# Attention with residual on one core: the fourth query product by a second level of Strassen's scheme, and half of the last scores queued behind the values

## The chip, the cores and the metric

One core of a Trainium2 chip runs the whole program. The metric is the device time in microseconds (us) of one execution. The kernel before has a median of 1027.39 us over three runs (1027.23 to 1027.47). 0.2% of that, about what a measurement can tell from no change, is 2.05 us.

## The reference, cut to what is computed

Multi-query attention with 16 heads of 64 and one shared key/value head, over 64 batches of 128 tokens of 512 numbers, all float32, with a layernorm ahead and one behind, and the input added at the end:

```python
xn = layernorm(x, g_in)                                  # x: (64, 128, 512)
q = (xn @ Wq).reshape(b, n, 16, 64) * 64**-0.5           # Wq: (512, 1024)
k, v = split(xn @ Wkv)                                   # 64 + 64 columns
k, v = [null_k; k], [null_v; v]                          # one extra position
sim = einsum('bhid,bjd->bhij', q, k) + bias              # bias: (16, 128, 128) and a null column
attn = softmax(where(causal and not masked, sim, -big))
out = einsum('bhij,bjd->bhid', attn, v).reshape(b, n, 1024) @ Wo
x + layernorm(out, g_out)
```

## The kernel before, in words

**Work in steps.** The batches are taken in pairs, 32 steps `d` of two batches `a = 2d` and `b = 2d + 1`; four batches make a group `g`, so a group lasts two steps (`h = 0` in the even, `h = 1` in the odd one). A step is `turn(d)` (L956) followed by `body(d)` (L1245). `turn` puts out the scores of `a` and `b` (L652), adds the bias to them on DVE (L667) and multiplies the softmax of the pair before with its values (L781). `body` computes the keys and values (L363, `pkv`) and half of the queries of the group that comes next, the output projection of the pair before (L868, tiles `py`), the rest of the softmax (row maxima L674 on DVE, exponentials L683 on ACT, reciprocals L701 on DVE, scaling L705 on POOL, transposition in blocks of 32, `blocks_T`, L721 on DVE), and the outgoing layernorm of an earlier pair. Queries end with `d = 29`: `d = 30` and `31` are `turn_end` (L984) and `body_end` (L1099), and `turn_end(32)` with `body_last` (L1163) closes the program. Work of a group ahead of the first step is called the head, what stands behind `d = 29` the tail.

**What sets the order.** The schedule is written by hand: the order of the calls in the program is the order in each engine's queue. An engine takes its instructions in that order, and a later one does not pass one that waits. So moving a call moves its place on every engine that it uses, DMA issues on SP included.

**Query products.** `xn @ Wq` for a group is a product of two by two blocks: the token side is cut by batches (first two, last two) and by halves of the 512 inputs, the weight side by halves of the inputs and by halves of the 1024 outputs. Strassen's scheme in Winograd's form (`product`, L499) takes seven block products in place of eight, with sums of tokens (`token_sum`, on POOL, tiles `xS1` to `xS4`) and sums of weights (`wS`). One block product for 128 outputs (an `f`; two a step) is two matmuls of 256 columns. The seven go to the PSUM tiles `a` and `c`; ACT copies partial sums out (`keep`, L527), and DVE (`q_out`, L536) or ACT (`q_out` without a name, L533) writes the queries `qT`. Products 1, 6, 7 and 4 go to `a`, where 6, 7 and 4 are added to what stands there; 5 and 3 go to `c`.

**The second product** is already cut once more by the same scheme: `inner_product` (L565, matmul L581, tile `pl`) is seven single matmuls of 128 columns for both `f` of a step, in the PSUM tag `w`, and `inner_out` (L590, L597) seven additions of 128x128 on DVE. Its token sums `xL` come from POOL (L561) and its weight sums `wL` are made once.

**PSUM** has eight banks here: `s` (two), `a` and `c`, `X` and `Y`, and two of `w`. A tile that is allocated waits until the tile that had the bank has been read.

**Values.** `values` (L761) multiplies the transposed softmax with the values in four strips of 32 rows, each with its own quarter of the key positions and two column halves of the array, in four turns; a strip's matmul is 256 columns in the first turn and 128 in the other three. An argument `wide`, not used before, lets a strip take the two blocks of its third value tile as one matmul of 256 columns.

**Output projection.** `out_product` (L850) is the same scheme on the other side: products 1 to 7, each four matmuls of 256 columns, with sums made by `out_sum` (L848), and results put together by `out_keep` (L880) and `out_part` (L896, L898).

## Time and profile before

| | |
|---|---|
| median of three runs | 1027.39 us |
| time of the profiled execution | 1027.63 us |
| span in its trace | 1025.8 us |
| lies outside the span | 1.8 us |
| granted TensorE clock, mean | 0.999 |

In the profile every float32 matmul shows as two records, and so does its weight load; a group "x8" of L868 is thus one `out_product` of four matmuls. Where rows of matmuls follow one another, the time from one start to the next is what a group costs the queue; the second column is longer, because matmuls are pipelined and the last one's way through the array is counted. PE is the engine of the matmuls, PEld that of weight loads (beside PE), DVE, ACT and POOL work on vectors, SP issues DMAs. A bracket such as `[0.61 <-DVE oT L798]` says that the engine stood for 0.61 us ahead of the row and that the DVE instruction of line 798 ended this.

### The profile page before, as it was taken

To read this page: it belongs to the slowest core of one execution; us is meant where nothing else is said; L and a number is where in the kernel's file an instruction comes from. 1 tells how busy PE (TensorE), PEld (TensorE's weight loads), DVE (VectorE), ACT (ScalarE), POOL (GpSimd) and SP (SyncE) were. 2 spreads that over 40 slices of the span, in tenths; PEclk is the share of its full clock that TensorE was granted. 3 is DMA by queue.
4 is the path that set the end of the run, shared out by engine and by line. 5 is a ranking of instruction groups with operands and counts; after the bars stand their busy time and mean duration, and the time that the engine had idled before them with its cause. 6 is when DMAs were issued, how large, how long until landed. Compare 5 with 4: busy or idle time off the path is not lost.

```text
span 1025.8 us, 31271 instructions
## 1 busy us (share of the span) xinstructions
PE 1016.4 (99%) x12345; PEld 898.9 (88%) x12345; DVE 800.4 (78%) x1774; ACT 697.4 (68%) x2805; POOL 744.7 (73%) x579
## 2 busy tenths in 40 slices
PE   9999999999999999999999999999999999999997
PEld 9888888888888888888888888888888888888886
DVE  6877788877778877788777888777887777877697
ACT  5765678666677666786666776666776667856582
POOL 4997768676686867759677686766868678586676
PEclk9999999999999999999999999999999999999999
DMA  7415243051431414224052330514314152140211
GB/s 217 139 30 150 69 117 120 30 155 64 143 97 66 125 56 150 89 81 137 29 165 74 109 123 26 165 63 138 103 51 130 64 151 89 70 113 21 88 64 62
DMA packets 73833, 100.84 MB, mean 98 GB/s; under 512 B 32212, under 2 KB 36056, under 8 KB 71896
## 3 DMA queue, kind: packets, MB, share of 16 engines
q1 hardware_dynamic: 73392, 98.47, 30.9%
q8 instruction: 96, 1.57, 0.7%
q14 instruction: 49, 0.40, 0.1%
q10 hardware_dynamic: 296, 0.40, 0.1%
HBM read 63.19 MB, written 33.55 MB: 94 GB/s over the span
## 4 chain that ended last, share of the span: by engine, by line
PE 97%; DVE 1%; POOL 1%; issue 0%; POOLq 0%; DVEq 0%; ACT 0%
PE pa L515 20%; PE pyX L868 19%; PE pyY L868 10%; PE pc L515 10%; PE po L781 7%; PE pkv L363 6%; PE pyw L868 5%; PE pl L581 4%; PE pq L450 3%; PE ps L652 3%; PE sc_X L652 2%; PE sc_Y L652 2%; PE py_s L868 1%; PE sc_a L652 1%; PE busy L1453 1%; PE sc_w L652 1%
## 5 line engine op out<-in xcount | busy, mean ns | idle before, releaser
L683 ACT ACTIVATE s<-s,nmax 128x65 f32<-128x65 f32 (+1 forms) x1024 | 372.2, 368 | 62.1 <-DVE nmax L674 62.0
L705 POOL TENSOR_TENSOR s<-s,rinv 128x512 f32<-128x512 f32 (+1 forms) x132 | 190.6, 1446 | 159.9 <-DVE rinv L701 159.9
L617 POOL TENSOR_TENSOR s<-biasp,mneg 128x1552 f32<-128x1552 f32 (+1 forms) x65 | 206.0, 3171 | 51.1 <-DVE s L667 38.1
L683 ACT ACTIVATION_READ_ACCUMULATOR s<-s,nmax 128x1 f32 x1024 | 195.4, 191 | 0.0
L533 ACT COPY qT<-pa 128x256 f32<-128x256 f32 x59 | 22.0, 373 | 147.7 <-PE pa L515 147.7
L674 DVE TENSOR_REDUCE nmax<-s 128x8 f32<-128x1032 f32 (+1 forms) x128 | 121.4, 949 | 0.1
L515 PE MATMUL pa<-xS,wq 128*128 128x256 f32 x472 | 121.2, 379 | 0.0
L721 DVE STREAM_TRANSPOSE sb<-s 128x1536 f32<-128x1536 f32 (+1 forms) x68 | 113.5, 1672 | 2.0 <-POOL s L705 2.0
L868 PE MATMUL pyX<-wo,oT 128*128 128x256 f32 x464 | 109.7, 379 | 0.0
L868 PE MATMUL pyX<-wT,oT 128*128 128x256 f32 x464 | 109.7, 379 | 0.0
L515 PEld LDWEIGHTS pa<-xS,wq 128*128 128x128 f32 x472 | 87.3, 190 | 11.0 <-issue 0.2
L868 PEld LDWEIGHTS pyX<-wo,oT 128*128 128x128 f32 x464 | 86.0, 190 | 10.5
L868 PEld LDWEIGHTS pyX<-wT,oT 128*128 128x128 f32 x464 | 85.9, 190 | 10.6
L848 POOL TENSOR_TENSOR oT<-oT 128x512 f32<-128x512 f32 x64 | 80.5, 1276 | 3.9 <-PE pyw L868 1.6
L781 PE MATMUL po<-sb,vr 32*64 32x256 f32 (+1 forms) x4064 | 81.0, 300 | 0.0
L781 PEld LDWEIGHTS po<-sb,vr 32*64 32x64 f32 x4064 | 70.9, 130 | 8.1 <-issue 5.7
L536 DVE TENSOR_TENSOR qT<-pc,ku 128x256 f32<-128x256 f32 x118 | 48.6, 412 | 35.9 <-PE pc L515 20.8
L597 DVE TENSOR_TENSOR qT<-pl,kp 128x128 f32<-128x128 f32 x112 | 31.3, 280 | 55.5 <-PE pl L581 52.9
L800 ACT ACTIVATE oT<-po,nv 128x512 f32<-128x512 f32 (+1 forms) x127 | 73.8, 655 | 0.1
L281 POOL TENSOR_TENSOR rstd<-rstd,nhalf 128x1 f32<-128x1 f32 x64 | 35.0, 554 | 42.1 <-DVE rstd L280 39.2
L527 ACT COPY ku<-pa 128x256 f32<-128x256 f32 x118 | 43.4, 368 | 30.2 <-PE pa L515 26.2
L363 PE MATMUL pkv<-xT,wkv 128*128 128x256 f32 x256 | 63.3, 391 | 0.0
(186 smaller groups left out, 2418.9 us busy)
## 6 DMA issues: line engine op xcount, KB each, us to landing
res<-in_x_dram SPq DMA_DIRECT2D x64, 256.0 KB
x<-in_x_dram SPq DMA_DIRECT2D x63, 256.0 KB
out_dram<-y SPq DMA_DIRECT2D x63, 256.0 KB
xd<-xb SPq DMA_DIRECT2D x14, 1024.0 KB
xT<-xd SPq DMA_DIRECT2D x56, 256.0 KB
vr<-vd SPq DMA_DIRECT2D x64, 128.0 KB
kT<-kT SPq DMA_DIRECT2D x32, 64.0 KB
vd<-vb SPq DMA_DIRECT2D x32, 64.0 KB
```

Of the source, the lines that this page charges most:

```text
L363: nc.tensor.matmul(pkv, wkv[:, kc, :], xT[g][:, t : t + 2, kc, :], start=(kc == 0), stop=(kc == KC - 1),)
L515: nc.tensor.matmul(prod[tag], w[:, kc, f * P : (f + 1) * P], t[:, :, kc, :], start=(start and kc == 0), stop=(kc == HK - 1), skip_group_ch ...
L617: nc.gpsimd.tensor_tensor(S[b][:, :, keys], biasp[:, :, keys], mneg[:, t, keys] .unsqueeze(1) .broadcast_to([P, R8, keys.stop - keys.start ...
L652: nc.tensor.matmul(home[r][u * DH : (u + 1) * DH, f, :], qT[g, f, t // 2][rows, t % 2, hf, u], kT[rows, 0 : nk // Q, t, :], start=True, st ...
L674: nc.vector.tensor_reduce(nmax[b][:, hf], S[b][:, :, WITH_NULL[hf]], AX.X, ALU.max, negate=True)
L683: nc.scalar.activation(row, row, AF.Exp, bias=nmax[b][:, hf, k : k + 1], accum_out=rsum[b][:, hf, k : k + 1],)
L705: nc.gpsimd.tensor_tensor(sv, sv, rinvs[b, hf][:, lo:hi].unsqueeze(2).broadcast_to([P, hi - lo, sv.shape[2]]), ALU.mult,)
L721: nc.vector.transpose(sbs[b][:, :, lo:hi].rearrange("p j e q -> p e j q"), S[b][:, lo:hi, 1 : ROW - 1].rearrange("p e (j k) -> p e j k", k=Q),
L781: nc.tensor.matmul(po[s][rows, to : to + n], vr[g][quad, t, PLACE[j], :], sb[quad, slots, r * NF : (r + 1) * NF, :], start=(turn == 0), st ...
L800: nc.scalar.activation(to, src, AF.Identity, bias=nv2)
L848: eng.tensor_tensor(o, a, b, op)
L868: nc.tensor.matmul(prod[key], h[:, c, :], w[:, c, :], start=(start and c == 0), stop=(c == HC - 1), skip_group_check=not start,)
```

## The change

Four things change, and some memory is rearranged for them.

**1. The fourth product of steps 4 to 29 is cut once more.** For both `f` of a step, `product(g, f, 4)` (two matmuls of 256 columns each, added in the bank `a`, then an ACT copy to `qT`) goes. In its place stand seven matmuls of 128 columns (`last_product`, L647 of the kernel after, tile `pm`, in the two banks `s`), each of them a product of token sums and weight sums, and seven additions of 128x128 on DVE (`last_out`, L663). The partial result that was in the bank is now taken from the copies that `keep` had already made (`base`). In each even step POOL makes four more token sums (`token_sums_last`, tile `xM` and one block of `xS4` in place), and DVE makes four weight sums once, in steps 2 and 3.

**2. Calls are reordered around it.** `product(g, f1, 1)` moves up to where product 4 of `f0` stood. Products 5 and 3 of `f1` change places with output products 5 and 7. `scale(a, 1)` stands ahead of `values_T`.

**3. Wide values.** In `turn` of steps 5 to 29, strip 3 of `values(p)` takes its third value tile as one matmul of 256 columns; `values(p + 1)` does in odd steps and in those with `d % 10 == 4`.

**4. The last steps.** In `turn_end` of 30 and 31 the second half of the scores of `b` moves from ahead of the values to behind them, with other PSUM banks; `exps(a, 0)` is cut at 4 of 8 heads, with `scores_max(b, 0)` and `out_sum(p, 0)` between. In `body_end` of 30 the second half of `blocks_T(b)` no longer waits for the next turn, and two `late_gain` go from DVE to POOL.

Besides: one `x` tile fewer is loaded ahead (`XB`), the mask tile of a group has one buffer and its load moves from the even to the odd step, and the head computes one of its query blocks as four matmuls of 256 columns (`q_half(7, 0)`) where it had eight of 128.

```diff
+    def last_product(g, h, k):
+        if k == 1:
+            last_in[g, h] = ps_s.tile([P, 2, DIM], FP, tag="s", name=f"pm_{g}_{h}")
+        b, x = xS[g, 4], xM[g]
+        w, t, at = {
+            1: (g11, b[:, 0, 0], 0),
+            2: (g12, b[:, 0, 1], 2),
+            3: (v4, b[:, 1, 1], 1),
+            4: (g22, x[:, 2], 0),
+            5: (v1, x[:, 0], 1),
+            6: (v2, x[:, 1], 0),
+            7: (v3, b[:, 1, 0], 0),
+        }[k]
+        nc.tensor.matmul(last_area(g, h, at), w[:, h], t, start=k in (1, 2), ...)
+    def last_out(g, h, f, t, at, first=False):
+        o = q_part(g, HC + 2 * h + f, 0)[:, t]
+        p = last_area(g, h, at).rearrange("p (h i) -> p h i", h=2)
+        k = o
+        if first:
+            k = base[f].rearrange("p (t h i) -> p t h i", t=2, h=2)[:, t]
+        nc.vector.tensor_tensor(o, p, k, ALU.add)
...
-        values(p)
-        values(p + 1)
+        values(p, WIDE if 4 < d < PAIRS - 1 else ())
+        values(p + 1, WIDE if 4 < d < PAIRS - 1 and (d % 2 or d % 10 == 4) else ())
...
-        scores(b, 1, ((ps_y, "X"), (ps_q, "c")))
...
-        po = values_rooms(p)
+        values_rooms(p, ((ps_q, "c"), (ps_w, "w"), (ps_y, "X"), (ps_w, "w")))
         values(p)
         values(p + 1)
+        scores(b, 1, ((ps_y, "Y"), (ps_q, "a")))
...
         if soft:
             scale(b, 0)
+        if sums and d > 2:
+            token_sums_last(g)
...
-        if q:
+        if deeper:
+            product(g, f1, 1, ps_q, "a")
+        elif q:
             product(g, f0, 4, ps_q, "a", start=False)
             q_out(g, HC + f0, 0, "a")
...
+        if deeper:
+            product(g, f1, 3, ps_q, "c", start=False)
+            q_out(g, f1, 1, "c", "u2")
+            last_product(g, h, 3)
+            last_product(g, h, 4)
+            last_out(g, h, 1, 0, 0, True)
+            last_out(g, h, 0, 1, 1)
         if soft:
             blocks_T(b)
-        if q:
+        if q and not deeper:
             product(g, f1, 4, ps_q, "a", start=False)
             q_out(g, HC + f1, 0, "a")
```

**How the queues change.** A row below is one instruction or a run of equal ones ("x2"); the figures in a name are group, `f` or `h`, product and a running number. First TensorE's queue in the middle of the odd step of group 12 (`d = 23`), before: `pl` is the second product, `pa` and `pc` the block products, `pyY` the output product 5.

```order
L581 MATMUL pl_12_1_9996<-xT_12_9254,wq_81 128x128
L515 MATMUL pa_12_2_1_9989<-xS4_12_9616,wq_81 128x256 x2
L515 MATMUL pc_12_2_5_10031<-xT_12_9254,wS_139 128x256 x2
L515 MATMUL pa_12_3_1_10089<-xT_12_9254,wq_81 128x256 x2
L581 MATMUL pl_12_1_9996<-xL_12_9559,wq_81 128x128
L515 MATMUL pc_12_3_5_10116<-xS1_12_9520,wS_139 128x256 x2
L868 MATMUL pyY_44_5_10119<-wT_141,yS_44_10011 128x256 x4
L515 MATMUL pa_12_3_1_10089<-xS2_12_9522,wS_139 128x256 x2
```

The same place after; `pm` is the new tile:

```order
L581 MATMUL pl_12_1_10155<-xT_12_9396,wq_81 128x128
L515 MATMUL pa_12_3_1_10222<-xT_12_9396,wq_81 128x256 x2
L515 MATMUL pc_12_2_5_10190<-xT_12_9396,wS_138 128x256 x2
L647 MATMUL pm_12_1_10250<-xS4_12_9763,wq_81 128x128 x2
L581 MATMUL pl_12_1_10155<-xL_12_9708,wq_81 128x128
L936 MATMUL pyY_44_5_10277<-wT_140,yS_44_10170 128x256 x4
L515 MATMUL pc_12_3_5_10284<-xS1_12_9669,wS_138 128x256 x2
L515 MATMUL pa_12_3_1_10222<-xS2_12_9671,wS_138 128x256 x2
L581 MATMUL pl_12_1_10155<-xL_12_9708,wq_81 128x128
L581 MATMUL pl_12_1_10155<-xT_12_9396,wL_139 128x128
L647 MATMUL pm_12_1_10250<-xM_12_9805,wM_92 128x128 x2
```

The product of `xS4` for `f = 2` (two matmuls of 256) is gone; `pa` of `f = 3` stands in its place, two `pm` matmuls of 128 follow, and the output product 5 passes ahead of `pc` of `f = 3`.

Second, DVE's queue at the end of the same step, before (`sb` is the transposed softmax, and the last row is the first score addition of the next step):

```order
L536 TENSOR_TENSOR qT_12_3_1_9947<-pc_12_3_5_10116,ku3_10153 128x4x64
L898 TENSOR_TENSOR y_44_10049<-pyY_44_5_10119,kyu2_10146 128x256
L536 TENSOR_TENSOR qT_12_3_1_9947<-pc_12_3_5_10116,ku2_10129 128x4x64
L904 BN_STATS sto_44_10166<-y_44_10049 128x6
L906 BN_AGGR mvo_44_10168<-sto_44_10166 128x2
L908 TENSOR_SCALAR rstdo_44_10170<-mvo_44_10168 128x1
L898 TENSOR_TENSOR y_45_10177<-pyX_44_1_10013,kyp5_10124 128x256
L721 STREAM_TRANSPOSE sb_47_10179<-s_47_9745 128x8x6x32
L667 TENSOR_TENSOR s_48_9928<-sc_48_0_w_10190,s_48_9928 128x4x64
```

After:

```order
L536 TENSOR_TENSOR qT_12_3_1_10104<-pc_12_3_5_10284,ku3_10317 128x4x64
L663 TENSOR_TENSOR qT_12_3_0_10103<-pm_12_1_10250,ku3_10317 128x2x64
L663 TENSOR_TENSOR qT_12_3_0_10103<-pm_12_1_10250,qT_12_3_0_10103 128x2x64
L966 TENSOR_TENSOR y_44_10208<-pyY_44_5_10277,kyu2_10310 128x256
L972 BN_STATS sto_44_10330<-y_44_10208 128x6
L974 BN_AGGR mvo_44_10332<-sto_44_10330 128x2
L976 TENSOR_SCALAR rstdo_44_10334<-mvo_44_10332 128x1
L966 TENSOR_TENSOR y_45_10341<-pyX_44_1_10172,kyp5_10282 128x256
L536 TENSOR_TENSOR qT_12_3_1_10104<-pc_12_3_5_10284,ku2_10290 128x4x64
L663 TENSOR_TENSOR qT_12_3_0_10103<-pm_12_1_10250,ku3_10317 128x2x64
L663 TENSOR_TENSOR qT_12_2_0_10101<-pm_12_1_10250,qT_12_2_0_10101 128x2x64
L787 STREAM_TRANSPOSE sb_47_10350<-s_47_9905 128x8x6x32
```

Four of the seven additions of a step now stand here, and the second addition from `pc` has moved behind the last one of the output (`y_45`), so that three instructions stand between that and the transposition.

Third, TensorE's queue in `turn_end` of step 30, before (`ps` and `sc` are scores, `po` the values' results):

```order
L652 MATMUL ps_60_1_12618<-kT_138,qT_15_3_0_12370 64x128 x4
L652 MATMUL sc_61_1_X_12635<-kT_138,qT_15_0_0_11991 64x128 x2
L652 MATMUL sc_61_1_c_12636<-kT_138,qT_15_0_0_11991 64x128 x2
L652 MATMUL sc_61_1_X_12635<-kT_138,qT_15_1_0_11993 64x128 x2
L652 MATMUL sc_61_1_c_12636<-kT_138,qT_15_1_0_11993 64x128 x2
L652 MATMUL sc_61_1_X_12635<-kT_138,qT_15_2_0_12368 64x128 x2
L652 MATMUL sc_61_1_c_12636<-kT_138,qT_15_2_0_12368 64x128 x2
L652 MATMUL sc_61_1_X_12635<-kT_138,qT_15_3_0_12370 64x128 x2
L652 MATMUL sc_61_1_c_12636<-kT_138,qT_15_3_0_12370 64x128 x2
L781 MATMUL po_58_0_12662<-sb_58_12531,vr_14_11736 64x2x128 x2
```

After:

```order
L849 MATMUL po_58_2_12861<-sb_59_12792,vr_14_11938 64x128 x2
L849 MATMUL po_58_3_12862<-sb_59_12792,vr_14_11938 64x128 x2
L718 MATMUL sc_61_1_Y_12927<-kT_137,qT_15_0_0_12189 64x128 x2
L718 MATMUL sc_61_1_a_12928<-kT_137,qT_15_0_0_12189 64x128 x2
L718 MATMUL sc_61_1_Y_12927<-kT_137,qT_15_1_0_12191 64x128 x2
L718 MATMUL sc_61_1_a_12928<-kT_137,qT_15_1_0_12191 64x128 x2
L718 MATMUL sc_61_1_Y_12927<-kT_137,qT_15_2_0_12576 64x128 x2
L718 MATMUL sc_61_1_a_12928<-kT_137,qT_15_2_0_12576 64x128 x2
L718 MATMUL sc_61_1_Y_12927<-kT_137,qT_15_3_0_12578 64x128 x2
L718 MATMUL sc_61_1_a_12928<-kT_137,qT_15_3_0_12578 64x128 x2
L936 MATMUL py_58_1_s_12984<-wo_90,oT_58_12952 128x256 x4
```

The sixteen `sc_61_1` matmuls now stand between the last matmul of the values and the first output product, `py_58_1_s` (`py_s` in the profile).

More of the change, by code (lines that the diff above doesn't have):

```diff
@@ L597, in inner_out, with weight_sums_last, token_sums_last, last_area @@
         nc.vector.tensor_tensor(o, p, k, ALU.add)
+    in_last = a22.rearrange("p k (h f m) -> p k f h m", h=2, f=2)
+    g11, g12 = in_last[:, 0, 0], in_last[:, 1, 0]
+    g21, g22 = in_last[:, 0, 1], in_last[:, 1, 1]
+    v1, v2 = (wM[:, i * 2 * P : (i + 1) * 2 * P] for i in range(2))
+    v1, v2 = (v.rearrange("p (h m) -> p h m", h=2) for v in (v1, v2))
+    v4, v3 = wR, g21
+    xM, last_in, base = {}, {}, {}
+    def weight_sums_last(*ks):
+        for k in ks:
+            o, p, m, op = {
+                1: (v1, g21, g22, ALU.add),
+                2: (v2, v1, g11, ALU.subtract),
+                4: (v4, g12, v2, ALU.subtract),
+                3: (v3, g11, g21, ALU.subtract),
+            }[k]
+            nc.vector.tensor_tensor(o, p, m, op)
+    def token_sums_last(g):
+        b = xS[g, 4]
+        x = xM[g] = gp.tile([P, 3, N], FP, tag="xM", name=f"xM_{g}", bufs=1)
+        for o, p, m in (
+            (x[:, 0], b[:, 1, 0], b[:, 0, 0]),
+            (b[:, 1, 0], b[:, 1, 1], b[:, 1, 0]),
+            (x[:, 1], b[:, 1, 1], x[:, 0]),
+            (x[:, 2], b[:, 0, 1], x[:, 1]),
+        ):
+            nc.gpsimd.tensor_tensor(o, p, m, ALU.subtract)
+    def last_area(g, h, at):
+        two = last_in[g, h]
+        return two[:, 0, 0:N] if at == 0 else two[:, 1, (at - 1) * N : at * N]
+    def last_product(g, h, k):
[10 more added lines that the diff above has]
+            7: (v3, b[:, 1, 0], 0),
+        }[k]
+        nc.tensor.matmul(
+            last_area(g, h, at),
+            w[:, h],
+            t,
+            start=k in (1, 2),
+            stop=True,
+            skip_group_check=k not in (1, 2),
+        )
+    def last_out(g, h, f, t, at, first=False):
[5 more added lines that the diff above has]
+        nc.vector.tensor_tensor(o, p, k, ALU.add)
     S, nmax, rsum = {}, {}, {}
@@ L1154, in body_end @@
         blocks_T(b, *lo)
-        late_T.append((b, *hi))
+        if last:
+            late_T.append((b, *hi))
+        else:
+            blocks_T(b, *hi)
+            for m in (l, l + 1):
+                late_gain(m, nc.gpsimd)
+                late_residual(m, nc.gpsimd)
         out_product(p, 4, ps_s, "s", start=False)
         out_part(p + 1, 0, "s")
-        if not last:
-            for m in (l, l + 1):
-                late_gain(m)
-                late_residual(m, nc.gpsimd)
     def body_last():
@@ L1255, in body @@
         deep = q and d > 1
+        deeper = q and d > 3
         if q:
@@ L1384, in body @@
             weight_sums_inner()
[L1385 to L1386 removed]
+        if d == 2:
+            weight_sums_last(1, 2, 4)
         if soft:
@@ L1391, in body @@
             exps(b, 1, 0, 2)
-        if q:
+        if q and h == 1:
+            values_T(g)
+        if q and not deeper:
             product(g, f1, 5, ps_q, "c")
@@ L1396, in body @@
             out_keep("Y", "yp5", "yp5")
+        if deeper:
+            product(g, f1, 5, ps_q, "c")
         if soft:
@@ L1406, in body @@
             inner_out(g, h, 0, 1, 1)
+        if deeper:
+            last_product(g, h, 6)
+            last_product(g, h, 5)
+            last_out(g, h, 0, 1, 0, True)
         if soft:
@@ L1425, in body @@
             out_part(p, 1, "Y", "yu2")
-        if q:
+        if q and not deeper:
             product(g, f1, 3, ps_q, "c", start=False)
```

69 lines of the change are left out of this document (40 added, 29 removed).

## The prediction

> **What bounds the kernel now.** I read the page first: the span, the busy shares, the granted clock and the shares of the chain that ended last.
>
> ```profile
> span 1025.8 us, 31271 instructions
> ...
> PE 1016.4 (99%) x12345; PEld 898.9 (88%) x12345; DVE 800.4 (78%) x1774; ACT 697.4 (68%) x2805; POOL 744.7 (73%) x579
> ...
> PEclk9999999999999999999999999999999999999999
> ...
> PE 97%; DVE 1%; POOL 1%; issue 0%; POOLq 0%; DVEq 0%; ACT 0%
> ```
>
> TensorE is busy 99% of the span and holds 97% of the chain, at a full clock from end to end. An average can hide stages, so next I cut two neighbouring steps out of the middle, each from one key/value product (`pkv`) to the next. The columns are the sum of the engine work in PE, PEld, DVE, ACT and POOL, then clock and DMA.
>
> ```profile
> 504.08:535.31 31.23, 31.23 (x388) 27.64 (x383) 25.00 (x57) 21.26 (x87) 21.69 (x16) 1.00 0.42 126
> 535.31:566.53 31.22, 31.22 (x386) 27.62 (x382) 24.27 (x56) 22.27 (x89) 23.60 (x20) 1.00 0.21 73
> ```
>
> PE works 31.23 of 31.23 us and 31.22 of 31.22: no wait is left in a step. Every other engine has four us or more to spare. So inside a step only the length of TensorE's own queue counts, as long as no other engine becomes late. That makes the forecast a count of matmuls, plus a search for new waits.
>
> **Part 1, the fourth product: what it costs on TensorE.** The timeline of PE in the first of these steps gives the price of both sizes. The columns are start and length; the queue's price is the distance between starts.
>
> ```profile
> 513.04 0.61 PE L581 MATMUL pl<-xL,wL 128*128 128x128 f32 x4
> 513.49 0.39 PE L581 MATMUL pl<-xT,wq 128*128 128x128 f32 x2
> 513.71 1.03 PE L515 MATMUL pa<-xS,wq 128*128 128x256 f32 x4
> 514.58 1.03 PE L515 MATMUL pc<-xT,wS 128*128 128x256 f32 x4
> 515.44 1.03 PE L515 MATMUL pa<-xT,wq 128*128 128x256 f32 x4
> 516.30 0.38 PE L581 MATMUL pl<-xL,wq 128*128 128x128 f32 x2
> ...
> 519.98 0.38 PE L581 MATMUL pl<-xL,wq 128*128 128x128 f32 x2
> 520.20 0.39 PE L581 MATMUL pl<-xT,wL 128*128 128x128 f32 x2
> 520.42 1.89 PE L868 MATMUL pyX<-wT,oT 128*128 128x256 f32 x8
> ...
> 527.33 1.03 PE L515 MATMUL pa<-xS,wq 128*128 128x256 f32 x4
> 528.20 1.89 PE L868 MATMUL pyX<-wT,oT 128*128 128x256 f32 x8
> ```
>
> Twelve records of 256 columns run from 513.71 to 516.30: 2.59 / 12 = 0.216 us each. Ten of 128 columns take 513.71 − 513.04 = 0.67 and 520.42 − 519.98 = 0.44, so 1.11 / 10 = 0.111 us each. The fourth product is the row at 513.71 for the first `f` and the one at 527.33 for the second: 8 records, 8 × 0.216 = 1.73 us of a step. In its place come seven matmuls, 14 records: 14 × 0.111 = 1.55 us. The saving is 0.173 us a step, and in 26 steps (4 to 29) **4.5 us**. A cut into seven of eight would save an eighth, 0.216; the small size gives 0.043 of that back.
>
> Do these small matmuls cost 0.111 here too? Their weight loads last longer than that:
>
> ```profile
> L581 PEld LDWEIGHTS pl<-xL,wq 128*128 128x128 f32 x112 | 21.3, 190 | 2.9
> ```
>
> 190 ns each, but the ten records above come 111 ns apart with these loads, so loads overlap one another, and `last_product` has the same sizes. I take 0.111, with bounds of 0.110 (the 0.44 over four) and 0.112 (the 0.67 over six), ± 0.014 a step, ± 0.4 us in all.
>
> **Part 1 elsewhere.** DVE gets seven additions a step, ACT loses two copies, POOL gets four subtractions in every second step:
>
> ```profile
> L597 DVE TENSOR_TENSOR qT<-pl,kp 128x128 f32<-128x128 f32 x112 | 31.3, 280 | 55.5 <-PE pl L581 52.9 <-ACT kp L527 1.8
> L533 ACT COPY qT<-pa 128x256 f32<-128x256 f32 x59 | 22.0, 373 | 147.7 <-PE pa L515 147.7
> L561 POOL TENSOR_TENSOR xL<-xT,xL 128x128 f32<-128x128 f32 x14 | 6.4, 457 | 1.1
> ```
>
> DVE: 7 × 0.28 = 1.96 us on top of 25.00, under 27 of 31.2. ACT: 2 × 0.373 = 0.75 less. POOL: 4 × 0.457 = 1.83 on top of 23.60, in an even step. All three keep 4 us or more, so only their places in the order can hurt. The tightest is the end of a step on DVE and POOL's `scale(b, 0)` in the even one:
>
> ```profile
> 527.53 0.42 DVE L898 TENSOR_TENSOR y<-pyX,kyp 128x256 f32<-128x256 f32 x1 [0.30 <-PE pyX L868]
> 527.88 1.77 DVE L721 STREAM_TRANSPOSE sb<-s 128x1536 f32<-128x1536 f32 x1
> ...
> 530.78 0.42 DVE L667 TENSOR_TENSOR s<-sc_w,s 128x256 f32<-128x256 f32 x1 [1.14 <-PE sc_w L652]
> ```
>
> ```profile
> 547.75 1.04 POOL L705 TENSOR_TENSOR s<-s,rinv 128x512 f32<-128x512 f32 x1
> 550.01 1.91 POOL L705 TENSOR_TENSOR s<-s,rinv 128x1024 f32<-128x1024 f32 x1 [1.21 <-DVE rinv L701]
> ```
>
> In the changed queue one output product stands between the last `pm` matmul and the scores, as the row at 528.20 does now. So the last `pm` leaves the queue at about 528.20 and is through the array 0.39 − 0.22 = 0.17 later, at 528.37; the last addition ends at 528.65 and the transposition at about 530.4, where it now ends at 529.65. The next score addition starts at 530.78 because of its matmul, and was idle for 1.14 us before that. About 0.35 us of it is left: no wait for PE. Behind that addition are the other scores, whose PSUM banks `w` the values need. What is queued behind a late transposition is just that, so each us beyond the 0.35, and beyond what the values leave, would be one of TensorE's. POOL's 1.83 us start where `scale(b, 0)` ends (551.92) and fall partly into the idle time that `scale(a, 1)` has ahead of it, as `scale(b, 0)` has 1.21; DVE transposes `a` after it, for values that come in the next step. `pm` needs `xM` only with its third matmul, 2 × 0.22 and a `pl` and two larger products later. I count nothing for these, and bound it by rival A.
>
> **Part 3, wide values.** Here a matmul of 256 columns replaces two of 128 in strip 3: 4 records fewer per call, 25 calls for `p` (steps 5 to 29) and 15 for `p + 1` (13 odd steps, 14 and 24), 40 calls.
>
> ```profile
> L781 PE MATMUL po<-sb,vr 32*64 32x128 f32 x3048 | 60.8, 271 | 0.0
> L781 PE MATMUL po<-sb,vr 32*64 32x256 f32 x1016 | 45.4, 389 | 0.0
> ```
>
> ```profile
> 501.63 2.52 PE L781 MATMUL po<-sb,vr 32*64 32x256 f32 x128
> 504.08 1.99 PE L363 MATMUL pkv<-xT,wkv 128*128 128x256 f32 x8
> ```
>
> A pair takes 504.08 − 501.63 = 2.45 us for 128 records. The eight corners of the array run side by side, and each has per batch 2 records of 256 and 6 of 128: 2 × 2 × 0.216 + 12 × 0.111 = 2.20 us for two batches. So columns explain 2.20 of 2.45, and the number of columns does not change. At most the remaining 0.25 comes from the count of records, 2.45 / 128 = 0.019 each, which would be 0.077 per call; at least nothing. I take the middle, 0.035 per call, as both limits are about equally near: 40 × 0.035 = **1.4 us** (0 to 3.1). What could be below nothing is rivals B and C.
>
> **Part 4, the tail.** The only other waits of PE that the change touches are these, before the first output product of the last two turns:
>
> ```profile
> PE py_s L868 <- DVE oT L798: 1.4, 2, 0.8
> ```
>
> ```profile
> 970.01 2.52 PE L781 MATMUL po<-sb,vr 32*64 32x256 f32 x128
> 973.14 1.97 PE L868 MATMUL py_s<-wo,oT 128*128 128x256 f32 x8 [0.61 <-DVE oT L798]
> ...
> 988.90 0.35 ACT L683 ACTIVATE s<-s,nmax 128x65 f32<-128x65 f32 x1 [2.87 <-DVE nmax L674]
> ...
> 992.00 1.97 PE L868 MATMUL py_s<-wo,oT 128*128 128x256 f32 x8 [0.79 <-DVE oT L798]
> ...
> 1002.61 0.80 ACT L1090 ACTIVATE y<-y,lnm,lrs 128x512 f32<-128x512 f32 x1
> ...
> 1003.66 1.91 DVE L721 STREAM_TRANSPOSE sb<-s 128x768 f32<-128x768 f32 x2
> ...
> 1005.62 0.45 PE L781 MATMUL po_s<-sb,vr 32*64 32x256 f32 x4
> ```
>
> Half of the scores of `b` now run in these waits of 0.61 and 0.79. But the last values (1005.62) start when the last transposition ends (1003.66 + 1.91 = 1005.57), and that is the end of ACT's exponentials, begun at 988.90 after a row maximum of the first scores of step 31. Those come 0.61 earlier at best, by the first wait; the second is off the path. `scores_max(b, 0)` and `out_sum(p, 0)` now stand between parts of the exponentials' inputs and outputs, which may cost some of it. I take **0.5 us**, between a loss of 0.3 and a gain of 1.4 (both waits). For the rest I count nothing: the head block has the same columns in fewer matmuls; the four weight sums (4 × 0.42 at most, as the 128x256 addition at 527.53) fall once into DVE's 6 us of idle time in a step; the mask load stands on SP behind the step's only reader of its one buffer, ahead of `x` loads that are needed a step later.
>
> **Sum.** 1027.63 − 4.5 − 1.4 − 0.5 = 1021.2 for the profiled execution; it lay 0.24 above the median of the runs, so **1021.0**. The bounds together: 4.9 + 3.1 + 1.4 gives 1018.0, and 4.1 + 0 − 0.3 gives 1023.6.
>
> **Rivals.**
>
> *A: the new additions make TensorE wait.* If DVE's end of a step is late by more than the 0.35 us and the slack of the banks, each step loses again what it won. For it: DVE's end of step has three instructions more ahead of a 1.77 us transposition. Against it: no PE wait for DVE is in either window. With 0.173 a step lost: 1027.4 − 1.4 − 0.5 = **1025.5**. Chance 0.09.
>
> *B: the wide matmul of strip 3 holds the other strips.* The queue's later records are for strips 0 to 2, which have finished with their 128 columns when strip 3 is in its second 128. If these must stand until strip 3 is through, both of its records cost the difference of the two rows above, 389 − 271 = 118 ns: 0.236 per call, 40 × 0.236 = 9.4 us. Time: 1027.4 − 4.5 − 0.5 + 9.4 = **1031.8**, slower. It decides from 5.0 / 40 = 0.125 us per call. For it: no row of before has records of both sizes in one turn. Against it: 128 records of 271 or 389 ns each go through in 2.45 us, so corners do run beside one another, and strip 3's second record has only to have started, not ended, for the queue to move on. Chance 0.07.
>
> *C: matmuls end in order.* If a short record may not end before a long one ahead of it, only the second record of strip 3 delays what follows, once per call: 40 × 0.118 = 4.7 us, time 1027.4 − 4.5 − 0.5 + 4.7 = **1027.1**, no change. No row of before shows a short record behind a long one. The Trainium skill has this rule, which speaks against the change: "TensorE: Matmul & The Clock Gate", Part 3: Packing small matmuls — row/col tiling, The mechanism, says that matmuls keep program order in start and in end. Chance 0.045.
>
> *D: it doesn't do what it says*, the small matmuls paying their whole load of 190 ns: 14 × 0.19 − 1.73 = 0.93 us a step more, 26 × 0.93 = 24 us, **1049**. The `pl` rows speak against it. Chance 0.02.
>
> **How the numbers follow.** The forecast has 0.775. A lies at the bound of 0.2% (2.05 us, about what a measurement of this kernel can tell from no change; 1025.3), so half of it counts as faster, half as the same. Faster: 0.775 + 0.045 = 0.82; same: 0.045 + 0.045 = 0.09; slower: 0.07 + 0.02 = 0.09. The range holds the forecast's bounds except their last few tenths below, and reaches up to A: 1018.6 to 1025.5.
>
> **What would show it.** `pm` rows 0.22 apart per two records, and `pkv` rows 31.05 instead of 31.23 apart, less up to 0.1 by the values, whose 2.45 becomes some 2.38. No PE row with idle time that DVE `qT` or `s`, or POOL `xM`, ended; such rows would be A. Values that last 2.6 or 2.7 in odd steps would be C or B. In the tail, `py_s` without its 0.61 and 0.79, and the last values about 6 us earlier than 1005.62. The prediction is wrong at its root if the distance of `pkv` rows does not shrink.

## The result, and the profile after

The changed kernel takes 1023.07 us (median of six runs, 1022.52 to 1023.66) where the kernel before takes 1027.41: a ratio of 0.9957, 95% interval 0.9946 to 0.9968. That is 4.3 us less; the forecast was 6.4 less (1021.0, range 1018.6 to 1025.5). The profiled executions differ by 1027.63 − 1022.89 = 4.74 us, and this is the difference that the views below take apart.

The page of the kernel after:

```profile
span 1021.0 us, 31459 instructions
...
PE 1013.0 (99%) x12333; PEld 901.6 (88%) x12333; DVE 845.7 (83%) x1958; ACT 673.2 (66%) x2753; POOL 768.6 (75%) x633
...
q8 instruction: 96, 1.57, 0.6%
...
PE 97%; POOL 1%; DVE 1%; issue 0%; ACT 0%; POOLq 0%; DVEq 0%
```

TensorE still sets the time. The row `q8` is new to the argument: it is the queue that brings TensorE's instructions, 96 packets of 1.57 MB / 96 = 16.4 KB. TensorE has 2 × 12,333 records (matmuls and weight loads), so a packet holds 24,666 / 96 = 257 of them; I take 256 below, and the places at which packets come will bear that out.

Two neighbouring steps without a stop (TensorE standing still in the middle of the values), and the two that had one (step 4, ending at 159.96, and step 16, ending at 533.00), in the columns of the prediction:

```profile
564.08:595.17 31.09, 31.09 (x390) 27.75 (x385) 26.73 (x64) 20.30 (x85) 20.77 (x16) 1.00 0.45 129
595.17:626.25 31.08, 31.08 (x386) 27.72 (x381) 25.96 (x63) 21.31 (x87) 26.12 (x24) 1.00 0.22 72
128.59:159.96 31.37, 31.37 (x388) 27.78 (x383) 25.45 (x58) 21.39 (x88) 21.84 (x16) 1.00 0.43 127
501.86:533.00 31.14, 31.14 (x391) 27.62 (x385) 26.78 (x64) 20.35 (x85) 20.85 (x16) 1.00 0.43 125
```

A step went from 31.225 to 31.09 and 31.08, where the forecast said 31.05 less up to 0.1. PE's share cannot show the stops, because the last group's modelled end covers them; the length of the window does: 31.37 and 31.14.

The new matmuls, the end of a step on DVE, and one pair's values with the key/value product that follows:

```profile
917.35 0.61 PE L647 MATMUL pm<-xS,wq 128*128 128x128 f32 x4
917.80 0.39 PE L581 MATMUL pl<-xL,wq 128*128 128x128 f32 x2
...
934.61 2.54 PE L849 MATMUL po<-sb,vr 32*64 32x256 f32 x120
937.07 1.13 PE L363 MATMUL pkv<-xT,wkv 128*128 128x256 f32 x4
```

```profile
930.35 0.28 DVE L663 TENSOR_TENSOR qT<-pm,qT 128x128 f32<-128x128 f32 x1
930.55 1.77 DVE L787 STREAM_TRANSPOSE sb<-s 128x1536 f32<-128x1536 f32 x1
932.53 0.42 DVE L733 TENSOR_TENSOR s<-sc_w,s 128x256 f32<-128x256 f32 x1 [0.21 <-PE sc_w L718]
```

`pm` costs (917.80 − 917.35) / 4 = 0.112 us a record, as forecast. The transposition ends at 932.32 and the score addition still waits for its matmul, with 0.21 us of idle time left (0.35 was forecast): DVE delays nobody. The values of this pair take 937.07 − 934.61 = 2.46 us, not less than the 2.45 of before.

The waits of PE in the whole program (the first row is the start):

```profile
PE busy L1556 <- POOL neg L245: 1.4, 1, 1.4
PE py_s L936 <- DVE rinv L767: 0.7, 2, 0.4
PE pyc L936 <- DVE y L966: 0.6, 1, 0.6
```

`py_s` before the first output products no longer waits for `oT`; two smaller waits, 0.28 and 0.38 us, stand at other places of the tail. And one wait of before is missing that the prediction did not speak of. In step 1, before and after:

```profile
85.15 1.89 PE L868 MATMUL pyY<-wo,oT 128*128 128x256 f32 x8
87.49 1.13 PE L515 MATMUL pc<-xT,wS 128*128 128x256 f32 x4 [0.45 <-DVE qT L536]
```

```profile
85.08 1.89 PE L936 MATMUL pyY<-wo,oT 128*128 128x256 f32 x8
86.80 1.03 PE L515 MATMUL pc<-xT,wS 128*128 128x256 f32 x4
```

From `pyY` to `pc` it was 2.34 us and is 1.72. On DVE the reciprocal of `a` now passes `values_T`, a transposition of 0.71 us; POOL's scaling, `blocks_T` and the addition that frees the bank `c` all come 0.9 us earlier.

**The first account.** By the starts of `pkv` the kernel after is 0.78 us ahead at step 2, and the steps and the tail give the rest. A theory from these views: the cut product gives what was forecast, wide values cost a little, the head and the tail give about 0.7 and 0.5. Its rivals stand with each run. The first runs showed that it lacked the most important thing.

### The profile page after: what moved, and what is told of

It reads as the page before. It is cut to its first block, busy times and chain, and to the rows that moved or that the text cites. A ratio compares the mean times of both kernels' runs of the same rounds, so it can differ in the third digit from the quotient of the medians.

```text
span 1021.0 us, 31459 instructions
## 1 busy us (share of the span) xinstructions
PE 1013.0 (99%) x12333; PEld 901.6 (88%) x12333; DVE 845.7 (83%) x1958; ACT 673.2 (66%) x2753; POOL 768.6 (75%) x633
## 3 DMA queue, kind: packets, MB, share of 16 engines
q8 instruction: 96, 1.57, 0.6%
## 4 chain that ended last, share of the span: by engine, by line
PE 97%; POOL 1%; DVE 1%; issue 0%; ACT 0%; POOLq 0%; DVEq 0%
PE pyX L936 20%; PE pa L515 16%; PE pyY L936 10%; PE pc L515 10%; PE po L849 8%; PE pkv L363 6%; PE pyw L936 5%; PE pl L581 4%; PE pm L647 4%; PE ps L718 3%; PE pq L450 3%; PE sc_X L718 2%; PE sc_Y L718 2%; PE sc_a L718 1%; PE py_s L936 1%; PE busy L1556 1%
## 5 line engine op out<-in xcount | busy, mean ns | idle before, releaser
L964 ACT COPY y<-pyX 128x256 f32<-128x256 f32 x29 | 10.8, 372 | 167.5 <-PE pyX L936 161.2
L849 PE MATMUL po<-sb,vr 32*64 32x128 f32 (+1 forms) x3904 | 81.8, 308 | 0.0
L515 PE MATMUL pa<-xS,wq 128*128 128x256 f32 x264 | 67.8, 380 | 0.0
L515 PE MATMUL pa<-xT,wq 128*128 128x256 f32 x236 | 60.6, 380 | 0.0
```

Source lines behind the costliest of these rows:

```text
L515: nc.tensor.matmul(prod[tag], w[:, kc, f * P : (f + 1) * P], t[:, :, kc, :], start=(start and kc == 0), stop=(kc == HK - 1), skip_group_ch ...
L849: nc.tensor.matmul(po[s][rows, to : to + n], vr[g][quad, t, PLACE[j], :], sb[quad, slots, r * NF : (r + 1) * NF, :], start=(turn == 0), st ...
```

## The experiments

Every run is measured against the kernel before on the same chip (medians 1027.41 to 1027.55). A stop, below, is time by which the values of a pair of batches take longer than 2.47 us, counted where they take over 2.50; without one they take 2.45 with plain and 2.47 to 2.48 with wide values.

### Without wide values

```diff
-    WIDE = (3,)
+    WIDE = ()
```

Expected: 

> The changed kernel with no wide values. Theory (read from the trace after: values last 2.466 us in steps with two wide calls and 2.479 in those with one, against 2.450 before): wide values cost 0.016 to 0.029 us a step, and without them each pair takes 2.45 again; 14 x 0.016 + 11 x 0.029 = 0.5 us less, 1022.5. Rival (the prediction's term): wide values save 0.035 us a call, and the busier DVE makes the pairs long; without them each pair takes over 2.50 and the time is 1024.4.

Measured: 1030.83 us (ratio 1.0031, interval 1.0021 to 1.0042), 7.8 us slower than with them, which neither theory allowed. Two steps of this kernel, and the values in the second:

```profile
191.62:222.68 31.06, 31.06 (x393) 27.68 (x389) 26.72 (x64) 20.27 (x85) 20.76 (x16) 1.00 0.47 128
600.61:632.31 31.70, 31.45 (x391) 27.81 (x389) 26.09 (x63) 21.54 (x87) 25.50 (x25) 1.00 0.23 71
```

```profile
597.50 1.37 PE L849 MATMUL po<-sb,vr 32*64 32x256 f32 x59
599.14 1.54 PE L849 MATMUL po<-sb,vr 32*64 32x128 f32 x69 [0.27 <-issue]
600.61 1.56 PE L363 MATMUL pkv<-xT,wkv 128*128 128x256 f32 x6
```

Some steps take 31.06, shorter than any of the changed kernel; others 31.7, and then TensorE stands in the middle of the values for "issue": it waits for nothing that the profile shows. In the waits this is

```profile
PE po L849 <- issue: 2.4, 7, 0.7
...
PE pkv L363 <- issue: 0.5, 1, 0.5
```

and by the lengths of all pairs, 18 of 29 have a stop, 8.5 us in all (one more, of 0.75 us, falls into a `pkv`). Within the turn a stop's place moves back by 12 to 14 records from step to step (record 503 in one, 489 and 477 in the next two; 373, 359 and 347 later), and it ends 1.2 to 1.5 us after a `q8` packet has landed. So TensorE had run out of instructions at the border of a packet. New theory: **the program of a step has to keep the packets' borders where the next packet comes in time.** Counted in the program's order (two records and two loads for each matmul), a step of the kernel before has 764 instructions, near three packets of 256. Seven matmuls of 128 for four of 256 make 776; wide values take 16 or 8 away: 760 and 768, about 764 on average.

This count leaves out TensorE's semaphore instructions, which the trace also has: 8 in two steps of the kernel before, 10 in two of the changed kernel. With them a step of the kernel before has 764 + 4 = 768, exactly three packets, and its packets do come at the same place of every step: the third starts 27.4 to 28.2 us after the start of the values in each of the steps 2 to 28. A step of the changed kernel without wide values has 776 + 5 = 781, 13 more than three packets, which is the 12 to 14 by which the stops move.

### Without the cut product

```diff
-        deeper = q and d > 3
+        deeper = False
```

(and none of its sums). Expected: 

> The changed kernel with the fourth product as it was before (two matmuls of 256 columns a step and f, ACT copies, none of the new sums), wide values, tail and the other orders kept. Theory: the body of a step is 0.164 us longer again in 26 steps, 4.3 us, and the stop of 0.14 us in step 4 goes: 1023.1 + 4.3 - 0.1 = 1027.2. Rival: the cut product gives less than that in the body because its additions delay something, and the time rises by 3 us or less, to 1026.

Measured: 1033.95 us (1.0060, 1.0046 to 1.0074), again far outside both. Its steps have 748 or 756 instructions, and 16 pairs have stops, 4.6 us in all, with wide values in place. So it isn't the form of the values that makes or mends a stop.

### The old tail

The functions `turn_end` and `body_end` are those of before. Expected: 

> The changed kernel with the last two steps (turn_end, body_end) as they were before. Theory: the waits of 0.61 and 0.79 us ahead of the first output product come back, of which the end feels 0.5: 1023.6. Rivals: the end feels both, 1.4 us, 1024.5; or nothing, since the exponentials set the end, 1023.1.

Measured: 1023.49 (0.9960, 0.9948 to 0.9973), 0.42 more; the wait of `py_s` for `oT` is back with 1.3 us in two. A difference this small lies within the two kernels' spreads, and the traces put the tail lower: from the `pkv` of step 29 to the start of the last matmul it takes 78.41 us here and 78.14 in the changed kernel, 0.27 us. The rest of what the profiled executions differ by, 1023.76 − 1022.89 = 0.87, is mostly stops: in steps 2 and 4 the values take 2.93 and 2.86 us here, 2.45 and 2.59 there, although the program is the same up to step 29. So stops at these two steps come and go from one execution to the next.

### The old order of values_T

```diff
+        if q and h == 1:
+            values_T(g)
         if soft:
             exps(a, 1, 4)
             rinv(a, 1)
             scale(a, 1)
             exps(b, 1, 0, 2)
-        if q and h == 1:
-            values_T(g)
```

Expected: 

> The changed kernel with values_T ahead of rinv(a, 1) and scale(a, 1) again, in every odd step. Theory: in step 1 the 0.71 us transposition of values_T delays the reciprocal, POOL's scaling, the transposition blocks_T and the addition that frees the bank c, so PE waits about 0.6 us again there, and in the other steps nothing changes: 1023.8. Rival: the head's gain of 0.7 us is from the changed head block or the mask load, and the time stays at 1023.1; or each odd step of the changed kernel needs the new order, 13 x 0.5 us, 1029.

Measured: 1024.27 (0.9967, 0.9955 to 0.9980), 1.2 more (1.6 in the profiled executions). The wait in step 1 is back:

```profile
87.21 1.13 PE L515 MATMUL pc<-xT,wS 128*128 128x256 f32 x4 [0.44 <-DVE qT L536]
```

and in this execution step 2 had a stop in the values as well (2.97 us in place of 2.45), and another of about 0.55 us came in the values of step 31. Without its stop, the way from the `pkv` of step 1 to that of step 2 is 32.62 − 0.52 = 32.10 us, as in the kernel before (32.10), where the changed kernel takes 31.39. The head's gain is this order, 0.71 us in step 1 alone.

### Wide values on the kernel before

```diff
-        values(p)
-        values(p + 1)
+        values(p, (3,) if 4 < d < PAIRS - 1 else ())
+        values(p + 1, (3,) if 4 < d < PAIRS - 1 and (d % 2 or d % 10 == 4) else ())
```

Expected: 

> The kernel before with the wide values of the changed kernel and nothing else. Theory (from the run without wide values, where the stops of TensorE lie in the values, move by a constant number of instructions from step to step and end 1.3 us after a packet of the instruction queue has landed): what counts is TensorE's instructions per step, 764 by the order of the program before and after on average, three packets of 256 being 768. Wide values alone take 12 a step away, the packet boundary moves through the burst of scores and values, and the time rises by 3 to 7 us, to 1030.5 to 1034.5. Rival 1: wide values cost only their own 0.016 to 0.029 us a step, 1027.9. Rival 2 (the prediction's term): 1026.0.

Measured: 1033.10 (1.0053, 1.0039 to 1.0067): slower by 5.6 us, as the packets say, with 15 stops of 4.6 us. Wide values alone are a loss.

### No wide values, three matmuls fewer

```diff
-    WIDE = (3,)
+    WIDE = ()
...
                 for r in range(2):
+                    if turn == 3 and r == 1 and s < skip:
+                        continue
...
         values(p, WIDE if 4 < d < PAIRS - 1 else ())
-        values(p + 1, WIDE if 4 < d < PAIRS - 1 and (d % 2 or d % 10 == 4) else ())
+        values(p + 1, skip=3 if 4 < d < PAIRS - 1 else 0)
```

Expected: 

> The changed kernel without wide values, but with three matmuls of the values' last turn left out in steps 5 to 29 (strips 0 to 2, second column half, of the second batch; these outputs are not computed). The longest strip has all its columns as before. Theory: TensorE's instructions per step come from 776 back to 764, so the stops in the values go and a pair takes 2.45 us: 1022.4 to 1022.9. Rival: wide values help by their form (fewer records in strip 3, or less waiting behind DVE), which this kernel does not have: 1029 to 1031, as without wide values.

Measured: 1023.28 (0.9957, 0.9945 to 0.9970), 7.6 us less than without wide values, by 12 instructions a step that TensorE does not have to fetch. (This kernel leaves out part of the values of every second batch, so it serves to find the cause and not as a version to use. The pairs without a stop take 2.45 us as with all matmuls.) Two of its steps, and the starts of `pkv` twelve steps apart:

```profile
564.89:595.96 31.07, 31.07 (x386) 27.68 (x383) 26.74 (x64) 20.30 (x85) 20.74 (x16) 1.00 0.45 129
595.96:627.02 31.06, 31.06 (x386) 27.67 (x383) 25.99 (x63) 21.29 (x87) 26.16 (x24) 1.00 0.23 72
```

```profile
564.89 0.48 PE L363 MATMUL pkv<-xT,wkv 128*128 128x256 f32 x1
...
937.64 0.70 PE L363 MATMUL pkv<-xT,wkv 128*128 128x256 f32 x2
```

(937.64 − 564.89) / 12 = 31.0625: a step with the cut product and plain values, all pairs at 2.45. Stops are left in steps 2, 4 and 16, 1.2 us, so its time isn't lower than that of the changed kernel.

### Half a packet ahead of the steps

```diff
     def q_half(c, h):
         pq = q_room(c, h)
-        q_mm(pq, c, h)
+        if h == 1:
+            for t in range(2):
+                q_mm(pq, c, h, slice(t, t + 1))
+        else:
+            q_mm(pq, c, h)
         q_copy(pq, c, h)
```

Expected: 

> The changed kernel with eight query blocks of the head as eight matmuls of 128 columns in place of four of 256: 128 more instructions on TensorE ahead of the steps, half a packet, at 0.05 us each block, 0.4 us; the steps are untouched. Theory: every step meets the packet boundaries half a packet away from now, as the middle steps of the run without wide values did, which lost 0.2 to 0.6 us each: 25 x 0.4 = 10, so 1033 (1028 to 1038). Rival: the number of instructions in a step matters, but not where a boundary falls, or instruction packets are not the cause at all: 1023.5.

Measured: 1028.22 (1.0006, 0.9997 to 1.0015): 5.1 us more with untouched steps, 18 stops of 4.5 us. The place of the borders counts; the size I had expected was twice too large.

### The head's block as before

```diff
-    q_half(7, 0)
+    q_batches((7,))
```

Expected: 

> The changed kernel with its one rewritten query block of the head as before (eight matmuls of 128 columns): 16 more instructions ahead of the steps, which puts the packet boundaries of step 4 where the kernel before has them. Theory: the stops of 0.14 us in step 4 and 0.05 in step 16 go, for 0.05 us of the block: 1022.9, and the runs lie closer together than 1022.5 to 1023.7. Rival: the stop in step 4 is from the weight sums of step 3 on DVE: it stays, 1023.1.

Measured: 1023.20 (0.9960, 0.9947 to 0.9974). The stop of step 4 is gone, as the packets say (2.45 us where it had 2.59, with the same weight sums on DVE). But step 16 stops for 0.73 us here:

```profile
501.57:533.38 31.81, 31.73 (x390) 27.91 (x385) 27.45 (x66) 20.57 (x86) 21.51 (x16) 1.00 0.44 125
```

so the median is the same.

### Neither the cut product nor wide values

The two edits `deeper = False` and `WIDE = ()` together. Expected: 

> The changed kernel without both: the fourth product as before and no wide values, so that TensorE's instructions per step are 764 again; tail, head block and the other orders stay. Theory: no stops from instruction packets, the body 0.164 us longer again in 26 steps; 1023.1 + 4.3 - 0.6 (wide values' own cost) - 0.1 (step 4) = 1026.6. So the fourth product alone would be slower than before by its packets (1030.8), wide values alone too (1033.1), and only both together faster. Rival: orders and tail alone already give most of the gain, or their stops stay: below 1025, or above 1028.

Measured: 1032.54 (1.0046, 1.0032 to 1.0060). The theory as it stood fails: with 764 instructions in every step, each even step stops. The number keeps the borders in place, but at a wrong place: there are 16 instructions fewer ahead of the steps than in the kernel before (the head's block). By the count of the table below its steps begin their values at places 189 and 192, those of the kernel before at 205 and 208, and those of the changed kernel from step 5 on at 199 to 215.

### The borders 48 instructions later

Three more blocks of the head (`q_batches((4,))`, `((5,))`, `((6,))`) become `q_half`. Expected: 

> The changed kernel with three more query blocks of the head in four matmuls of 256 columns in place of eight of 128: 48 instructions fewer ahead of the steps, so that each packet boundary comes 48 instructions later in a step. Theory: the packet that data transfers delay in even steps (steps 4 and 16 above all) is then needed later, the stops there go and the runs lie closer together; three times 0.05 us less in the head: 1022.6. Rival: at this place other steps stop (as the middle of the run without wide values did), 1026 or more; or the spread of the runs has another cause and nothing changes, 1023.1.

Measured: 1030.50 (1.0030, 1.0019 to 1.0040): wrong, and the direction with it. 23 pairs stop, 6.3 us in all. A later border asks for its packet later too. At the end of a step an instruction takes about 0.1 us (26 us for some 250), in the scores and values 0.01 (5.3 us for 512), so the request moves much more than the need: in step 7 the packet starts 1.25 us ahead of the first score in the changed kernel and 1.66 us behind it here.

### The same, wide values in three of four steps

```diff
+        wide = WIDE if 4 < d < PAIRS - 1 and d % 4 != 2 else ()
-        values(p, WIDE if 4 < d < PAIRS - 1 else ())
-        values(p + 1, WIDE if 4 < d < PAIRS - 1 and (d % 2 or d % 10 == 4) else ())
+        values(p, wide)
+        values(p + 1, wide)
```

Expected: 

> As the run with the boundary later, and wide values for both batches in three of four steps and none in the fourth (764 instructions on average as before). Theory: 19 steps at 0.016 us in place of 14 at 0.016 and 11 at 0.029: 0.25 us less again, 1022.3. Rival: the larger swing of 8 instructions up and 8 down from step to step brings stops back: 1023 or more.

Measured: 1032.61 (1.0045, 1.0032 to 1.0058): 25 stops of 7.6 us from the same wrong start, and what the pattern itself is worth can't be told from it.

### Neither, with the head's block as before

`q_batches((7,))` again, on the kernel without both. Expected: 

> The run without the cut fourth product and without wide values (1032.5, its even steps stop 0.14 to 0.7 us in the values), with the head's one query block in eight matmuls of 128 columns again: 16 more instructions ahead of the steps and 0.05 us. Theory: the boundary that made the even steps stop is met 16 instructions earlier, some 1.1 us before the scores begin as in the kernel before, so its packet is there in time; all stops go, and what is left against the kernel before is the head (0.7) and the tail (0.5): 1026.3. The fourth product with the wide values is then worth 3.2 us. Rival: the even steps stop for another reason, DVE or data, and 1032.5 stays.

Measured: 1027.30 (0.9996, 0.9987 to 1.0005), 5.2 us less by 16 instructions in the head. No pair has a stop. In the 2 us ahead of the scores of step 10, the DMA view of this kernel, and then of the one with 16 fewer:

```profile
q1 hardware_dynamic: 978, 0.50, 90.5%
q8 instruction: 1, 0.02, 3.3%
```

```profile
q1 hardware_dynamic: 1006, 0.51, 93.9%
q14 instruction: 1, 0.01, 1.1%
```

(`q14` is another instruction queue, with smaller packets.) The packet of `q8` starts 0.73 us ahead of the first score here. In the other kernel it starts 1.00 us behind it, and the values there take 349.04 − 346.18 = 2.86 us:

```profile
346.18 2.93 PE L849 MATMUL po<-sb,vr 32*64 32x256 f32 x128
349.04 1.13 PE L363 MATMUL pkv<-xT,wkv 128*128 128x256 f32 x4
```

The median stays 1.0 us above what was expected; in this execution TensorE stood once in the head:

```profile
56.16 1.10 PE L515 MATMUL pa<-xS,wq 128*128 128x256 f32 x4 [0.70 <-issue]
```

This one is not a packet's: no `q8` packet had landed for 14 us. A semaphore instruction of TensorE lasts from 53.77 to 56.10 there, and ACT's copy out of `pa` ends at 56.06, over a microsecond later than in the other kernels. So "issue" alone does not tell the two apart.

### The runs side by side

"Place" is the number of the instruction with which the values of a step begin, modulo 256, up to a constant that is the same for all kernels; a smaller number means a later border. Places count the matmuls, the weight loads and the semaphore instructions, the second column only the first two. Stops are those of the pairs of steps 1 to 29 in one profiled execution.

| kernel | matmuls and loads a step | with semaphores, mean of steps 5 to 28 | place, steps 4 and 28 | pairs with a stop, us | median, us |
|---|---|---|---|---|---|
| before | 764 | 768 | 205, 205 | 0, 0 | 1027.41 |
| after | 760 and 768 | 768.3 | 189 (step 5: 205), 205 | 2, 0.2 | 1023.07 |
| no wide values | 776 | 781 | 189 (step 5: 205), 245 | 18, 8.5 | 1030.83 |
| no cut product | 748 and 756 | 755.3 | 189, 149 | 16, 4.6 | 1033.95 |
| before, wide values | 748 and 756 | 755.3 | 205, 165 | 15, 4.6 | 1033.10 |
| no wide, three fewer | 764 | 769 | 189 (step 5: 205), 225 | 3, 1.2 | 1023.28 |
| half a packet ahead | 760 and 768 | 768.3 | 61, 77 | 18, 4.5 | 1028.22 |
| head's block as before | 760 and 768 | 768.3 | 205, 221 | 1, 0.7 | 1023.20 |
| neither | 764 | 768 | 189 (step 5: 192), 189 | 14, 4.5 | 1032.54 |
| borders 48 later | 760 and 768 | 768.3 | 141, 157 | 23, 6.3 | 1030.50 |
| 48 later, three of four | 760 and 776 | 769 | 141, 181 | 25, 7.6 | 1032.61 |
| neither, head's block as before | 764 | 768 | 205, 205 | 0, 0 | 1027.30 |

Only the five kernels that stand at 205 to 221 in step 5 and keep within one instruction of 768 go without stops in most steps, and the two of them that start at 205 with 768 have none. (The old tail and the old order of `values_T` leave count and place as in the changed kernel.) The same holds pair by pair, across all fourteen kernels: 233 pairs begin at places 192 to 239, and 5 of them have a stop; of the other 173, 135 have one. Kernels whose borders wander are among both: without wide values, the steps 5 to 7 and 24 to 26 pass through these places and take 2.45 us. What the place decides is when the packet comes. Among the pairs at places 180 to 235, those whose packet starts no later than 0.75 us after the first score have one stop in 227, those with a later packet 38 in 41.

## Why the prediction held, and where it failed

**The bound** was right: the time of a step is the length of TensorE's queue, and DVE, POOL and ACT stayed hidden with 1.7 us more work on DVE in a step (26.73 in place of 25.00).

**Part 1, 4.5 us: right, a little large.** A step without stops takes 31.0625 with the cut product and 31.225 without, both with plain values: 0.163 in place of 0.173, 4.2 us in 26 steps; with 0.112 us for a record of 128 columns, the upper bound, the sum gives 0.162. Rival A (additions that make PE wait) did not come: 0.21 us were left at the tightest place. Nor did D.

**Part 3, a gain of 1.4 us: wrong, sign included.** The pair with wide values takes 2.46 to 2.48, not 2.38; steps of 31.08 and 31.09 against 31.06, 0.5 us of loss in 25 steps. The columns had explained 2.20 us and I gave the remainder to the count of records; fewer records did not shorten it. Rivals B and C, 0.118 or 0.236 a call, are excluded too: 0.03 a step is all. The Trainium skill's rule that matmuls keep the order of their ends ("TensorE: Matmul & The Clock Gate", Part 3: Packing small matmuls — row/col tiling, The mechanism) would have cost the 4.7 us of rival C; no such hold shows in these lengths. (The ends themselves are modelled in the profile, so this speaks against the price and not against the order.)

**What the forecast lacked is what wide values do here.** They give back instructions. The forecast counted what a matmul takes on the array and nothing for fetching it, and the time stays in the range only because part 3 brings the count back to about 764 a step (768 with the semaphores). Part 1 without part 3 makes the kernel 3.3 us slower than before, head and tail included; part 3 alone, forecast at −1.4, makes it 5.6 slower; all together make it 4.3 faster. None of my rivals has this mechanism, so that the range held is luck in this part: the forecast leaves out a cost of several us, and wide values were counted on for another reason.

**Part 4, 0.5 us: the right way, about half the size**, 0.27 by the traces with the old tail and the new (0.42 by the medians, which stops blur). Both waits for `oT` are gone, but two others of 0.28 and 0.38 came, and the last values begin 4.6 us earlier (1001.04 in place of 1005.62), not 6. **"For the rest I count nothing": wrong for the head.** The order of `values_T` gave 0.71 us in step 1, by a wait of PE (0.45) that I had taken as untouched by the change.

**The sum** of the profiled executions: 4.2 (cut product) − 0.5 (wide values) + 0.8 (head, 0.78 at step 2) + 0.3 (tail) − 0.2 (stops of steps 4 and 16, 31.37 − 31.225 and 31.14 − 31.09) = 4.6. The spans differ by 1025.8 − 1021.0 = 4.8; the last 0.27 of it lies behind the last output, in closing instructions (6.05 us from the start of the last matmul to the end before, 5.78 after), which no part of the change touches.

**What stays open.** Why the packet of step 16 comes late with the cut product: it starts 0.78 to 1.10 us after the first score in the changed kernel and in four others (three matmuls fewer, head's block as before, old tail, old order of `values_T`; stops of 0.73, 0.65, 0.05 or none), but 0.33 and 0.15 us ahead of it in the two with 768 and the place 205. How many packets TensorE can hold is open too. That stops make the spread of the changed kernel's six runs, 1.1 us against 0.3 before, is argued; what is shown is that two executions of the same steps (changed kernel, old tail) differ by 0.75 us in the stops of steps 2 and 4. No version beat the changed kernel. 16 instructions in its head, what one block moves, changed nothing (1023.20); the same 16 were worth 5.2 us in the kernel with neither part.

## What to carry to other kernels

Where TensorE has no idle time and the program is one long stream, its instructions are a cost of their own: count them per step, semaphore instructions included, compare with a multiple of the 256 of a packet, and see where the borders fall against the densest stretch. An edit that is measured alone may look bad because it moves a border, so try it with the count restored. The mark of it is a wait for "issue" in the middle of equal matmuls, at a place that wanders from step to step when the count is off, and with an instruction packet that landed just before the wait ended (1.2 to 1.5 us here). The last condition is needed: the wait in the head of the last run had no such packet.

## What the runs showed of the hardware

A burst of scores and values is 512 instructions in 5.3 us, two packets, while the rest of a step takes 26 us for 250. A stop ends 1.2 to 1.5 us after its packet has landed (in the run without wide values, by the packets' own records), and lasted 0.04 to 0.93 us. In the run with 764 matmuls and loads and the wrong place, the data queue is at 84% or more in the 2 us ahead of the scores in every even step and idle in the odd ones from step 3 on; the packet starts 0.90 to 1.39 us after the first score in the even steps, up to 0.68 in the odd ones, and all stops are in even steps. Part of this is the place itself, 3 instructions or some 0.3 us; that the data transfers make the rest is likely and not shown. The Trainium skill ("Runtime: NRT & Kernel Launch", Instruction fetch mechanics) has the size right, blocks of 16 KiB with 256 instructions, where this trace has 16.4 KB and 257 records. It calls the crossing of a border mostly hidden; here up to 8.5 us of 1031 were not.
